# A closing phase of its own for the last graph, and four weight differences moved behind a norm

## The chip, the cores and the metric

The kernel runs on one core of one Trainium2 chip. The metric is the device time in microseconds (us) of one execution; the median of three runs is given. A profile is one further execution, taken by the hardware profiler, with a time of its own.

## What is computed

64 graphs of 256 nodes with 512 features pass two layers. Each layer normalizes its input, applies a relu, runs attention that a 256x256 mask per graph restricts, and adds the result to the input. Cut to what matters:

```python
h = relu(layernorm(x))                               # layer 0, 8 heads of 64
m = h @ map_w.T;  n = heads(m) / norm(heads(m))
q, k = heads(m @ q_w.T), heads(m @ k_w.T)
p = softmax(where(mask, NEG, q @ k.T / 8)) * keep
a = (n @ n.T > 0.1) * not_mask * p                   # "cosine" threshold
x = x + relu((a @ heads(h @ gcn_map_w.T)) @ gcn_W.T / (a.sum(-1) + 1))
h = relu(layernorm(x))                               # layer 1, 4 heads of 64
q, k, v = h @ Wq, h @ Wk, h @ Wv
x = x + (softmax(where(mask, q @ k.T / 8, -max)) @ v) @ Wo + bo
```

In layer 0 `mask` is where the adjacency is set (edges are taken out); in layer 1 only edges are kept. The softmax is computed without a maximum; sums are kept in `chk`, and at the end a branch takes a general path if one is out of bounds. With these inputs it is not taken.

## The kernel before, in words

All work on a graph is on whole tiles of 128 partitions, with keys on partitions and queries along the row, so that attention needs no transposes. The order of instructions on each engine is the order of the calls in the source: nothing is moved by a scheduler. Every engine works off its own queue in that order and waits for the others by semaphores.

`period(i)` is one step of a software pipeline over the graphs. In it stand, woven together: layer 1's attention of graph i-1 (called `b`), layer 0's attention and layer 1's norm and q, k, v of graph i (`g`), layer 0's products of graph i+1 (`nx`) and the normalized, transposed input of graph i+2 (`n2`). A loop runs `period` for i from 0 to 64. In period 63 there is no `nx`, and in period 64 only `b`, graph 63, is left.

The parts that the change and the prediction's steps touch:
- `products` (L404) makes scores on TensorE, `exps` (L411) exponentials on ScalarE (ACT), two banks of PSUM per pair of heads, from a ring of eight banks. `masked` multiplies by the mask on VectorE (DVE), L420 for layer 0 and L418 (edges) for layer 1.
- `halves` (L424) adds the two halves of a row of exponentials on GpSimd (POOL) to `d`, so that the sum product on TensorE has half the length.
- `units` (L387) makes unit vectors `nT`, for which the norms come back from DRAM; `cosines` (L441) makes their products, one triangle only. `far_off` masks by the threshold (L454, DVE), writes the off-diagonal block as `up` (L451, ACT) and has a DMA transpose it into `far` (L457); `far_back` masks the mirrored block by it (L466, DVE). `far_added` and `far_back` add both halves of the masked rows to `d` on POOL (L461, L468), but not for the last graph: there `sums` (L484) reads `d` and the two halves of `e`.
- `values` makes av (L431) and its relu (L474). `sums` gives `sms` by an ACT copy with a running sum (L486). `sums_back` transposes it (rt, L492) and takes reciprocals (L494); `heads_back` transposes avs (p_l), scales (L507) and adds to `xs` on POOL (L509).
- `moments` (L197 to L200), `deviations` (L203: root on ACT, then L204) and `normalized` (L210) are the second norm; `turned` transposes xn (p_t, L219) and writes hT with a relu (L220). L674 brings back the ACT table of the exponential.
- `queries_keys1` makes layer 1's q and k by seven half-size products (p_qk, L279), whose left factors POOL adds (L257 to L260) and whose results DVE adds (L304, L324); `values_in` makes v (p_v, L523).
- Of layer 1's attention: `sums1` (zb, L542) gives the softmax's denominators, one row per head; their reciprocals (L547) go through DRAM (`by_head`: by_rz, then `own`) to stand on all 64 partitions of a head; `values1` makes av1 (copied by L532), `divided` multiplies (L551), `result` makes p_o (L556) and adds it (L557); then the graph is stored.

The seven products need differences of weight blocks, which `finish_seven` makes in place by four DVE subtractions:

```python
sub(t[:, 5], t[:, 2], t[:, 3])      # L88
sub(t[:, 3], t[:, 3], t[:, 0])      # L89
sub(t[:, 4], t[:, 2], t[:, 3])      # L90
sub(t[:, 6], t[:, 1], t[:, 4])      # L91
```

For layer 1's weights `wqk1` this is called in period 0, behind the far blocks and ahead of the values of graph 0.

Of the kernel before, what the change touches and what calls it, by code (L numbers as in the profile page):

```python
# [150 lines left out]
def fast_path(ctx, tc, a, w, chk, out):  # L151
# [30 lines left out]

    def load(i):
        g = Graph()
        g.i, g.last, g.e, g.d, g.far = i, i == B - 1, {}, {}, {}
        g.xs = io.tile([P, NT, D], F32, tag="xs", name=f"xs{i}")
        nc.sync.dma_start(out=g.xs, in_=x_t[i])
        g.ad = io.tile([P, NT, S], U8, tag="ad", name=f"ad{i}", bufs=3)
        nc.sync.dma_start(out=g.ad, in_=adj_t[i])
        return g  # L190
# [194 lines left out]
    def units(g):  # L385

        nc.vector.tensor_mul(g.nT, g.nT, g.mT)  # L387
# [68 lines left out]
        g.far[c] = sb2.tile([P, 2, P], BF16, tag="far", name=f"far{g.i}_{c}", bufs=4)  # L456
        nc.sync.dma_start_transpose(out=g.far[c], in_=up.rearrange("p s q -> p (s q)"))  # L457

    def far_added(g, c):
        if not g.last:  # L460
            nc.gpsimd.tensor_add(g.d[c], g.d[c], g.e[c][:, :, :S])  # L461

    def far_back(g, c):

        e = g.e[c][:, :, S:S + P]
        nc.vector.scalar_tensor_tensor(e, g.far[c], 0.0, e, op0=ALU.is_gt, op1=ALU.mult)  # L466
        if not g.last:
            nc.gpsimd.tensor_add(g.d[c], g.d[c], g.e[c][:, :, S:])  # L468

    def values(g, n):  # L470
        av = bank(f"av{g.i}_{n}")
# [1 line left out]
            weighed(av, c - 2 * n, g.sem, g.e[c], 2 * c)  # L473
        nc.scalar.activation(g.avs[:, 2 * n:2 * n + 2, :], av, AF.Relu)  # L474

    def sums(g):

        sm = bank(f"sm{g.i}", [P, S])
        for n in range(2):
            for m in range(1 + NT if g.last else 1):  # L480
                for k in range(4):
                    c, s = 2 * n + k // 2, k % 2
                    part = g.e[c][:, s, (m - 1) * S:m * S] if m else g.d[c][:, s, :]
                    nc.tensor.matmul(sm[32 * k:32 * (k + 1), :], w.two[:, n, :], part, start=(n == 0 and m == 0),  # L484
                                     stop=(n == 1 and m == (NT if g.last else 0)))
        nc.scalar.activation(g.sms, sm, AF.Copy, accum_out=chk[:, g.i, 0:1])  # L486

    def sums_back(g):

# [25 lines left out]
        g.q1T, g.k1T = qk[:, :NIC, :], qk[:, NIC:, :]  # L515
        return seven_products(left, w.wqk1, None, qk, f"p_qk1{g.i}")

    def values_in(g, t):
        if t == 0:
            g.v = sb1.tile([P, NT, INNER], F32, tag="v", name=f"v{g.i}")  # L520
            g.p_v = bank(f"p_v{g.i}", [P, NT, INNER])
        for c in range(NKC):
            nc.tensor.matmul(g.p_v[:, t, :], g.h1T[:, c, t * P:(t + 1) * P], w.wv1[:, c, :],  # L523
                             start=(c == 0), stop=(c == NKC - 1))
        if t == NT - 1:
            nc.vector.tensor_copy(g.v, g.p_v)

    def values1(b):
        av = bank(f"av1_{b.i}")
        for c in range(NIC):  # L530
            weighed(av, c, b.v, b.e1[c], 2 * c)
        nc.scalar.copy(b.avs1, av)  # L532

    def sums1(b):

        zb = bank(f"zb{b.i}", [P, S])
        last = NT - 1 if b.last else 0
        for m in range(last + 1):
            for h in range(H1):
                c, s = divmod(h, 2)  # L540
                part = b.e1[c][:, s, m * S:(m + 1) * S] if b.last else b.d1[c][:, s, :]
                nc.tensor.matmul(zb[32 * h:32 * (h + 1), :], w.ones[:, :32], part, start=(m == 0), stop=(m == last))  # L542
        own = sb1.tile([P, 2, NIC, S], F32, tag="qk1", name=f"own{b.i}")
        b.avs1, b.z = own[:, 0], own[:, 1]
        b.rz = sb1.tile([P, S], F32, tag="rz", name=f"rz{b.i}")
        nc.scalar.activation(b.rz, zb, AF.Copy, accum_out=chk[:, b.i, 2:3])
        nc.vector.reciprocal(b.rz, b.rz)  # L547
        by_head(b.rz, 32, b.z, f"rz{b.i}")

# [7 lines left out]
        nc.vector.tensor_add(b.xs[:, t, :], p, b.xs[:, t, :])  # L557

    def period(i):
        g = graphs.get(i) if i < B else None  # L560
        b, nx, n2 = graphs.get(i - 1), graphs.get(i + 1), graphs.get(i + 2)
        def off_edges(*cs):
            for c in cs if g else ():
                masked(g.e[c], g.mask, edges=False)

        def halved_sums(*cs):
            for c in cs if g else ():
                g.d[c] = halves(g.e[c], f"0_{i}_{c}")


        if b:
            b.e1 = [exps(products(b.k1T, b.q1T, c, f"sc1_{b.i}_{c}"), f"1_{b.i}_{c}") for c in range(NIC)]
        if g:
            for c in range(NKC):
                g.e[c] = exps(products(g.kT, g.qT, c, f"sc0_{i}_{c}"), f"0_{i}_{c}")
        if b:
            for c in range(NIC):
                masked(b.e1[c], b.mask, edges=True)
            if b.last:
                for t in range(NT):  # L580
                    values_in(b, t)
        if nx:
            m, s = mapped(nx), messages(nx)
            next(m)
            next(s)

        off_edges(0, 1)
        halved_sums(1, 0)
        if b and not b.last:
            b.d1 = [halves(b.e1[c], f"1_{b.i}_{c}") for c in range(NIC)]  # L590
        if g:
            units(g)
        if nx:
            next(m)
        off_edges(2)
        halved_sums(2)
        if nx:
            next(m)
            next(s)
            next(m)  # L600
            halved(nx)

        if g:
            for c in range(NKC):
                far_off(g, c, cosines(g, c))
                if c == 0:
                    off_edges(3)
                    halved_sums(3)
            for c in range(NKC):
                far_added(g, c)  # L610
        if n2:
            shifts(n2, f"0_{n2.i}")
        if nx:
            q = queries(nx)
            next(q)
            next(s)
        if n2:
            sent(n2, f"0_{n2.i}", 0)
        if nx:
            next(q)  # L620
            squares(nx)
            next(s)
        if n2:
            sent(n2, f"0_{n2.i}", 1)
        for c in range(NKC):
            if nx and c < 3:
                next((q, s, q)[c])
            if g:
                far_back(g, c)
        if nx:  # L630
            lengths(nx, norms(nx))

        if i == 0:
            w.finish_seven(w.wqk1)
        if b:
            sums1(b)
            values1(b)
        if g:
            g.avs = sb1.tile([P, NKC, S], F32, tag="wide", name=f"avs{i}")
            g.sms = sb1.tile([P, S], F32, tag="sms", name=f"sms{i}")  # L640
            values(g, 0)
            values(g, 1)
            sums(g)
        if n2:
            joined(n2, f"0_{n2.i}")
            join(n2, 0)
        if nx:
            k = keys(nx)
            next(k)
        if b:  # L650
            nc.scalar.activation(b.rz, b.rz, AF.Copy, accum_out=chk[:, b.i, 3:4])
        if g:
            sums_back(g)
            heads_back(g)
        if n2:
            join(n2, 1)
        if nx:
            next(k)
        if n2:
            edges(n2)  # L660
        if b:
            divided(b)
        if g:
            moments(g, f"1_{i}")
        if nx:
            next(k)
        if g:
            deviations(g)
        if g:
            normalized(g, f"1_{i}")  # L670
        if nx:
            nc.scalar.activation(nx.rn, nx.rn, AF.Sqrt)

        nc.scalar.activation(spare[:, 1:], spare[:, :1], AF.Exp)  # L674
        if b:
            for t in range(NT):
                result(b, t)
                if b.last:
                    nc.sync.dma_start(out=out_t[b.i][:, t], in_=b.xs[:, t])
            if not b.last:  # L680
                nc.sync.dma_start(out=out_t[b.i], in_=b.xs)
        if i + 3 < B:
            graphs[i + 3] = load(i + 3)
        if g:
            g.h1T = turned(g, f"1_{i}", "wide")
            j = queries_keys1(g)
            for t in range(NT):
                nc.gpsimd.tensor_add(g.xs[:, t, :], g.xs[:, t, :], w.bo_b)
        if nx:
            next(k)  # L690
        if g:
            next(j)
        if nx:
            nc.vector.reciprocal(nx.rn, nx.rn)
            spread(nx)
        if g:
            next(j)
        if g:
            next(j)
            if not g.last:  # L700
                values_in(g, 0)
            next(j)
        if n2:
            n2.left_h = left_factors(n2.hT, "sh", n2.i)
        if i + 3 < B:
            moments(graphs[i + 3], f"0_{i + 3}")
        if g and not g.last:
            values_in(g, 1)

    def normal_input(g):  # L710
        g.hT = turned(g, f"0_{g.i}", "hT")
# [2 lines left out]
    with tc.manual_schedule():  # L714
# [54 lines left out]
            graphs[1].left_h = left_factors(graphs[1].hT, "sh", 1)  # L769
        if B > 2:  # L770
            moments(graphs[2], "0_2")
        for i in range(B + 1):
            period(i)


@with_exitstack
# [295 lines left out]
```

## Time and profile before

| | us |
|---|---|
| median of 3 runs | 3650.06 (3648.68 to 3650.47) |
| the profiled execution | 3652.85 |
| its span, first to last instruction | 3651.0 |
| PE busy in the span | 3613.9 (99%) |
| DVE, POOL, ACT busy | 2680.1, 2229.8, 1902.7 |
| weight loads (PEld) busy | 3088.9 |

The span is what the trace covers; the rest of the execution's time lies around it. PE is TensorE's products, PEld its weight loads, which run beside them. A row of the timeline gives start, length, engine, line, operation, tiles and number of instructions merged; in brackets, how long the engine had been idle just before and what released it. "PEclk" is the share of full speed that the throttle granted to TensorE. In a table of stretches, "(x…)" behind a busy time is the number of instructions. Every fp32 product stands in the trace as two records.

The middle periods are alike. The end of the program differs: period 63 begins near 3576 us of the span, period 64 near 3624 us.

### The profile page before, as it was taken

Reading aid. Unit: us, or ns where it says so; the run is one execution under the profiler, and the core shown is the slowest. Engines: PE = TensorE matmul, PEld = TensorE weight load, DVE = VectorE, ACT = ScalarE, POOL = GpSimd, SP = SyncE. Lnnn points to the kernel's source line nnn. Section 1 sums busy time; section 2 is a strip of 40 time slices with the busy share of each in tenths; the row PEclk is TensorE's granted clock in tenths of the full one; section 3 lists DMA queues with packets and bytes.
Section 4 is the critical chain, followed back from the end, with each engine's and each line's share of the span. In section 5 each row is a group of like instructions: output and inputs, shape, how many; then the busy total and the mean of one; then the engine's idle time right before and its main releaser. Section 6 shows DMA issues by size and latency. Waiting matters only on the chain.

```text
span 3651.0 us, 76421 instructions
## 1 busy us (share of the span) xinstructions
PE 3613.9 (99%) x29153; PEld 3088.9 (85%) x29153; DVE 2680.1 (73%) x5287; ACT 1902.7 (52%) x4481; POOL 2229.8 (61%) x2050
## 2 busy tenths in 40 slices
PE   8999999999999999999999999999999999999997
PEld 7888888888888888888888888888888888888885
DVE  7777777777777777777777777777777777777774
ACT  4555555555555555555545555555555555555542
POOL 4656656566566566665665666656656666566562
PEclk9999999999999999999999999999999999999998
DMA  4121121111211211211112112111121121211211
GB/s 118 44 57 44 55 56 46 55 51 50 57 44 55 61 42 54 53 50 56 45 54 61 44 52 57 46 56 45 53 61 44 53 57 47 55 45 54 60 32 33
DMA packets 358928, 191.73 MB, mean 53 GB/s; under 512 B 270336, under 2 KB 324896, under 8 KB 358560
## 3 DMA queue, kind: packets, MB, share of 16 engines
q1 hardware_dynamic: 357824, 186.24, 18.9%
q8 instruction: 233, 3.82, 0.4%
q14 instruction: 135, 1.11, 0.1%
q10 hardware_dynamic: 544, 0.52, 0.0%
q0 software_dynamic: 192, 0.04, 0.0%
HBM read 94.67 MB, written 34.34 MB: 35 GB/s over the span
## 4 chain that ended last, share of the span: by engine, by line
PE 97%; DVE 1%; DMA 1%; POOL 0%; issue 0%; ACT 0%; SPq 0%; ACTq 0%; DVEq 0%; POOLq 0%
PE sc L404 9%; PE av L431 9%; PE p_q L279 7%; PE p_m L279 7%; PE p_qk L279 6%; PE p_k L279 6%; PE p_o L556 6%; PE p_v L523 6%; PE p_s L274 6%; PE co L441 5%; PE p_qk_z L279 5%; PE p_m_z L279 5%; PE p_q_z L279 5%; PE p_k_z L279 5%; PE p_s_z L274 4%; PE sm L484 2%
## 5 line engine op out<-in xcount | busy, mean ns | idle before, releaser
L424 POOL TENSOR_TENSOR d<-e 128x512 f32<-128x512 f32 x382 | 595.7, 1584 | 366.2 <-DVE e L420 366.2
L411 ACT ACTIVATE e<-sc 128x512 f32<-128x512 f32 x768 | 383.3, 652 | 383.1 <-PE sc L404 376.8
L468 POOL TENSOR_TENSOR d<-d,e 128x512 f32<-128x512 f32 x252 | 322.8, 1291 | 171.4 <-DVE e L466 171.4
L509 POOL TENSOR_TENSOR xs<-xs,o 128x512 f32<-128x512 f32 x128 | 188.0, 1491 | 341.1 <-DVE o L507 341.1
L257 POOL TENSOR_TENSOR sh<-hT 128x256 f32<-128x256 f32 x128 | 93.3, 729 | 479.4 <-ACT hT L220 288.5
L420 DVE TENSOR_TENSOR e<-e,mask 128x1024 f32<-128x1024 f32 x256 | 378.8, 1500 | 0.0
L454 DVE SCALAR_TENSOR_TENSOR e<-co,e 128x256 f32<-128x256 f32 (+1 forms) x1024 | 287.8, 346 | 64.5 <-ACT up L451 35.4
L461 POOL TENSOR_TENSOR d<-d,e 128x512 f32<-128x512 f32 x252 | 312.5, 1272 | 0.0
L451 ACT ACTIVATE up<-co,below 128x128 bf16<-128x128 f32 x512 | 159.9, 363 | 186.2 <-PE co L441 180.4
L556 PE MATMUL p_o<-wo,own 128*128 128x512 f32 x512 | 236.1, 605 | 9.8 <-DVE own L551 9.8
L523 PE MATMUL p_v<-wv,hT 128*128 128x256 f32 x1024 | 242.2, 380 | 0.0
L431 PE MATMUL av<-e,sem 128*64 128x256 f32 x2048 | 232.4, 379 | 1.2 <-DVE e L466 1.2
L404 PE MATMUL sc<-qT,kT 64*128 64x256 f32 x2048 | 231.8, 377 | 0.0
L404 PEld LDWEIGHTS sc<-qT,kT 64*128 64x128 f32 x2048 | 198.4, 187 | 22.8 <-ACT hT L220 0.3
L494 DVE RECIPROCAL r<-rt 128x16 f32<-128x16 f32 x64 | 16.5, 258 | 268.5 <-PE rt L492 268.5
L431 PEld LDWEIGHTS av<-e,sem 128*64 128x64 f32 x2048 | 146.7, 137 | 76.1 <-DVE e L466 2.1
L523 PEld LDWEIGHTS p_v<-wv,hT 128*128 128x128 f32 x1024 | 185.1, 191 | 20.0 <-issue 0.3
L234 ACT ACTIVATE xn<-xs,shift,rs 128x512 f32<-128x512 f32 x124 | 100.5, 810 | 192.9 <-POOL d L461 190.4
L197 DVE BATCH_NORM_STATS2 st<-xs 128x6 f32<-128x512 f32 x256 | 173.9, 679 | 25.1 <-POOL xs L509 21.7
L466 DVE SCALAR_TENSOR_TENSOR e<-far,e 128x256 f32<-128x256 bf16 x256 | 190.3, 763 | 0.0
L441 PE MATMUL co<-nT 64*128 64x256 f32 (+1 forms) x2048 | 186.4, 332 | 2.8 <-ACT e L411 2.8
L556 PEld LDWEIGHTS p_o<-wo,own 128*128 128x128 f32 x512 | 94.5, 195 | 105.7 <-issue 102.4
(203 smaller groups left out, 9346.3 us busy)
## 6 DMA issues: line engine op xcount, KB each, us to landing
xs<-in_x_dram SPq DMA_DIRECT2D x64, 512.0 KB
nT<-by_rn SPq DMA_DIRECT2D x128, 256.0 KB
out_dram<-xs SPq DMA_DIRECT2D x63, 512.0 KB
own<-by_rz SPq DMA_DIRECT2D x128, 128.0 KB
ad<-in_adj_dram SPq DMA_DIRECT2D x64, 64.0 KB
far<-up SPq DMA_TRANSPOSE x256
turn<-flat SPq DMA_TRANSPOSE x248
mask<-adb SPq DMA_TRANSPOSE x128
```

Source lines behind the costliest of these rows:

```text
L274: nc.tensor.matmul(region, src[:, c, :], wt[:, block, c, :], start=p not in opened, stop=True, skip_group_check=True)
L279: nc.tensor.matmul(region[:, f, :], wt[:, block, c, f * P:(f + 1) * P], src[:, c, :], start=p not in opened, stop=True, skip_group_check=True)
L404: nc.tensor.matmul(ps[s][:, j, :], rows[h, c, j * P:(j + 1) * P], cols[h, c, :], start=True, stop=True)
L411: nc.scalar.activation(e[:, s, :], p.rearrange("p j q -> p (j q)"), AF.Exp, scale=SCALE)
L420: nc.vector.tensor_mul(e, e, m)
L424: nc.gpsimd.tensor_add(d, e[:, :, :S], e[:, :, S:])
L431: nc.tensor.matmul(av[s * DH:(s + 1) * DH, n, :], vs[:, j, (h0 + s) * DH:(h0 + s + 1) * DH], q[:, s, j * S:(j + 1) * S], start=(j == 0), s ...
L441: nc.tensor.matmul(ps[s][:, j, j * P:], g.nT[h, c, j * P:(j + 1) * P], g.nT[h, c, j * P:], start=(j == 0), stop=True, skip_group_check=True)
L461: nc.gpsimd.tensor_add(g.d[c], g.d[c], g.e[c][:, :, :S])
L468: nc.gpsimd.tensor_add(g.d[c], g.d[c], g.e[c][:, :, S:])
L523: nc.tensor.matmul(g.p_v[:, t, :], g.h1T[:, c, t * P:(t + 1) * P], w.wv1[:, c, :], start=(c == 0), stop=(c == NKC - 1))
L556: nc.tensor.matmul(p, b.avs1[:, c, t * P:(t + 1) * P], w.wo1[:, c, :], start=(c == 0), stop=(c == NIC - 1))
```

## The change

Three things change in the source:
- The loop runs `period` for i from 0 to 62, without its cases for missing graphs, and `closing()` follows. It does the work of periods 63 and 64: layer 0's attention of graph 63 (`g`), layer 1's of graph 62 (`b`) and then of graph 63, in an order of its own.
- `finish_seven(w.wqk1)` in period 0 stands behind `normalized(g)`.
- Helpers are cut differently (`sums` and `sums1` take a function that gives the parts to add, `inverted` and `own` are taken out of `sums1`, the copies of av1 and v go to the callers, `far_added` takes the half), with the same order of instructions in periods 1 to 62.

The diff's core:

```diff
-    def sums(g):
+    def sums(g, parts, name):
...
+        for c in range(NKC):
+            ps = parts(c)
+            for j, part in enumerate(ps):
+                for s in range(2):
+                    n, k = divmod(2 * c + s, 4)
+                    nc.tensor.matmul(sm[32 * k:32 * (k + 1), :], w.two[:, n, :], part[:, s, :],
+                                     start=(n == 0 and j == 0), stop=(n == 1 and j == len(ps) - 1))
+        return sm
...
-        if i == 0:
-            w.finish_seven(w.wqk1)
...
+        normalized(g, f"1_{i}")
+        if i == 0:
+            w.finish_seven(w.wqk1)
...
+    def closing():
+        g, b = graphs[B - 1], graphs.get(B - 2)
+        for c in range(NKC):
+            g.e[c] = exps(products(g.kT, g.qT, c, f"sc0_{g.i}_{c}"), f"0_{g.i}_{c}")
+        units(g)
+        co = [cosines(g, c) for c in range(2)]
+        for c in range(NKC):
+            masked(g.e[c], g.mask, edges=False)
+        se = sums(g, lambda c: both(g.e[c]), "se")
+        for c in range(2):
+            far_off(g, c, co[c])
+        first = sb1.tile([P, S], F32, tag="rn", name="first")
+        nc.scalar.activation(first, se, AF.Copy, accum_out=chk[:, g.i, 0:1])
+        for c in range(2, NKC):
+            far_off(g, c, cosines(g, c))
+        if b:
+            b.e1 = [exps(products(b.k1T, b.q1T, c, f"sc1_{b.i}_{c}"), f"1_{b.i}_{c}") for c in range(NIC)]
+        for c in range(NKC):
+            far_back(g, c)
+        if b:
+            for c in range(NIC):
+                masked(b.e1[c], b.mask, edges=True)
+        g.avs = sb1.tile([P, NKC, S], F32, tag="wide", name=f"avs{g.i}")
+        values(g, 0)
+        values(g, 1)
+        nc.scalar.activation(spare[:, 1:], spare[:, :1], AF.Sqrt)
...
+        nc.vector.tensor_add(g.sms, sums(g, lambda c: both(g.e[c]), "sm"), first)
+        sums_back(g)
+        heads_back(g)
+        if b:
+            sums1(b, lambda c: both(b.e1[c]))
+            own(b, "kT")
+            av = values1(b)
+        moments(g, f"1_{g.i}")
+        deviations(g)
+        if b:
+            nc.scalar.copy(b.avs1, av)
+        normalized(g, f"1_{g.i}")
+        nc.scalar.activation(spare[:, 1:], spare[:, :1], AF.Exp)
+        if b:
+            inverted(b)
+        g.h1T = turned(g, f"1_{g.i}", "wide")
+        j = queries_keys1(g)
...
+        next(j)
+        next(j)
+        next(j)
+        values_in(g, 0, (0, 1))
+        next(j)
+        values_in(g, 0, (2, 3))
+        g.e1 = [exps(products(g.k1T, g.q1T, c, f"sc1_{g.i}_{c}"), f"1_{g.i}_{c}") for c in range(NIC)]
+        values_in(g, 1)
+        nc.scalar.copy(g.v, g.p_v)
+        if b:
+            nc.scalar.activation(b.rz, b.rz, AF.Copy, accum_out=chk[:, b.i, 3:4])
+            divided(b)
+        for c in range(NIC):
+            masked(g.e1[c], g.mask, edges=True)
+        if b:
+            result(b, 0)
+        z = bank("z")
+        for c in range(NIC):
+            for j, part in enumerate(both(g.e1[c])):
+                for s in range(2):
+                    nc.tensor.matmul(z[s * DH:(s + 1) * DH, c, :], w.ones, part[:, s, :], start=(j == 0),
+                                     stop=(j == NT - 1))
+        spent = sb2.tile([P, NIC, S], F32, tag="xn", name="spent")
+        nc.scalar.activation(spent, z, AF.Copy, accum_out=chk[:, g.i, 2:3])
+        av = values1(g)
+        own(g, "qT")
+        for t in range(NT):
+            q = slice(t * P, (t + 1) * P)
+            nc.vector.reciprocal(g.z[:, :, q], z[:, :, q])
+            nc.vector.tensor_mul(g.avs1[:, :, q], av[:, :, q], g.z[:, :, q])
+        nc.scalar.activation(spent, g.z, AF.Copy, accum_out=chk[:, g.i, 3:4])
+        if b:
+            result(b, 1)
+            nc.sync.dma_start(out=out_t[b.i], in_=b.xs)
+        for t in range(NT):
+            result(g, t)
+            nc.sync.dma_start(out=out_t[g.i][:, t], in_=g.xs[:, t])
```

In the closing the last graph's denominators of layer 1 are made on all 64 partitions of each head at once (`z`, with 64 columns of ones), so they need no trip through DRAM. Layer 0's sum is made of two parts: `se`, of the edge-masked exponentials before the threshold, and `sm`, after it.

## The prediction

> **What bounds the kernel now.** I read the 40 slices first, then the chain that ended last, then the busy times by stage, then the timeline of the two places that the edit touches. The slices and the chain:
>
> ```profile
> PE   8999999999999999999999999999999999999997
> PEclk9999999999999999999999999999999999999998
> PE 97%; DVE 1%; DMA 1%; POOL 0%; issue 0%; ACT 0%; SPq 0%; ACTq 0%; DVEq 0%; POOLq 0%
> ```
>
> TensorE sets the time everywhere but in the last slice. Stage by stage (length, then PE, PEld, DVE, ACT, POOL busy, PEclk, DMA share, GB/s):
>
> ```profile
> 3456.00:3512.00 56.00, 56.00 (x456) 47.96 (x455) 41.49 (x83) 29.79 (x70) 34.84 (x33) 1.00 0.20 52
> 3568.00:3600.00 32.00, 26.55 (x226) 21.07 (x228) 20.56 (x35) 11.75 (x28) 14.34 (x11) 0.95 0.10 26
> 3600.00:3625.00 25.00, 20.14 (x128) 14.24 (x121) 10.48 (x22) 8.26 (x19) 8.20 (x8) 0.86 0.09 32
> 3625.00:3651.00 26.00, 11.77 (x53) 5.75 (x51) 7.13 (x11) 1.72 (x7) 0.00 (x0) 0.77 0.10 33
> ```
>
> A middle period is 56.0 us with PE full: nothing is to be had there. The last 75 us hold 16.5 us of idle PE, and part of the rest ran at half clock. The order of instructions on each engine is the same in both kernels except in period 0 and from the last graph's scores on, so only these two can move. The end of before:
>
> ```profile
> 3583.47 10.29 POOL L424 TENSOR_TENSOR d<-e 128x512 f32<-128x512 f32 x6 [11.41 <-DVE e L420]
> 3592.55 2.39 DVE L454 SCALAR_TENSOR_TENSOR e<-co,e 128x256 f32<-128x256 f32 x8 [1.32 <-POOL d L424]
> 3605.63 6.68 PE L556 MATMUL p_o<-wo,own 128*128 128x512 f32 x8 [2.43 <-DVE own L551]
> 3612.84 1.09 ACT L220 ACTIVATE hT<-p_t 128x512 f32<-128x512 f32 x2 [3.24 <-PE p_t L219]
> 3629.08 1.75 DVE L547 RECIPROCAL rz<-rz 128x256 f32<-128x256 f32 x1 [0.90 <-ACT rz L546]
> 3636.49 0.69 DVE L551 TENSOR_TENSOR own<-own 128x512 f32<-128x512 f32 x1 [2.63 <-DMA own<-by_rz]
> 3637.32 6.18 PE L556 MATMUL p_o<-wo,own 128*128 128x512 f32 x8 [7.00 <-DVE own L551]
> ```
>
> Three things make the end long: six half-sums on POOL that DVE's threshold masks wait for; graph 62's p_o standing on PE ahead of graph 63's transposes, at half clock; and graph 63's last normalization through DRAM (7.0 us of idle PE), after which p_o is at half clock again. The clock, read from PE alone (length, PE busy, clock):
>
> ```profile
> 82.27:85.69 3.42, 1.18 (x12) 1.00 0.09 22
> 85.69:89.10 3.41, 3.41 (x16) 0.50 0.54 162
> 3601.42:3604.83 3.41, 1.31 (x10) 1.00 0.18 60
> 3604.83:3608.24 3.41, 2.61 (x3) 0.50 0.00 0
> 3608.24:3611.65 3.41, 3.41 (x5) 0.50 0.03 5
> 3628.72:3632.13 3.41, 1.60 (x16) 1.00 0.00 1
> ```
>
> A stretch of 3.41 us with 1.2 or 1.3 us of PE work is followed by half clock, one with 1.6 is not; 2.6 busy us did not bring the full clock back, 3.4 did.
>
> **Part 1, weight differences in period 0.**
>
> ```profile
> 73.11 3.00 POOL L468 TENSOR_TENSOR d<-d,e 128x512 f32<-128x512 f32 x2 [0.43 <-DVE e L466]
> 73.55 1.43 DVE L88 TENSOR_TENSOR wqk<-wqk 128x512 f32<-128x512 f32 x1
> 75.01 1.64 DVE L89 TENSOR_TENSOR wqk<-wqk 128x512 f32<-128x512 f32 x1
> ```
>
> Alone one such subtraction takes 0.69 us (L90, L91); beside POOL's two sums the first two take twice that, and the sums take 3.00 us where period 62's take 2.56. PE's last sum product waited for that POOL result (0.64 us), and rt, the heads, the norm and the transposes follow it. Moved behind xn, the four run beside nothing of POOL: 4 x 0.69 = 2.8 us, from 85.5 to 88.3. Their reader is the second half of p_qk, at about 89.7. The kT additions behind them on DVE wait for p_k_z until 89.3, so they are not delayed. Gain 3.00 - 2.56 = 0.44 us; the bounds are 0 and 0.64 (the whole PE wait), and below nothing up to 1 us if p_k_z comes early. I take 0.44.
>
> **Part 2, the closing phase.** All times on before's clock; the anchor is 3576.41, where PE takes up scores. The half-sums (POOL 10.3 us), 8 products on d, and the last DRAM trip (3 DMAs) go; 16 products se, one ACT copy, one DVE addition, 8 products z, two reciprocals and two ACT copies come.
> - PE: scores of 63 first, 32 records, 3.62 us, to 3580.1. ACT's eight exps at 0.50 us (12 took 5.99) run from 3577.7 to 3581.85. nT had landed at 3576.0, so units (1.22) end at 3578.5, under the first exps. Four masks at 1.2 us follow ACT: to 3583.5. POOL is idle, so they stay at 1.2.
> - Cosines 0, 1 (half of 2.89): 3580.1 to 3581.5. se waits for the last mask. Eight sm products take 1.07 us (two records each), eight 64-row av products 1.95. The new order puts two products of one output group close together; I take 2.1 us for 16 if groups overlap across chunks, 3.4 if only pairs do. se ends at 3584.4, cosines 2, 3 at 3585.85, scores of 62 at 3587.7 (2.0 in before; here 1.85).
> - DVE: 16 threshold masks, 1.15 us a chunk, 3583.5 to 3588.1. The four DMA transposes of `far` land 2.36 us after their `up` and 1.25 to 1.35 us apart in before: the last at 3589.6. Four far_back (0.355) end at 3590.05; av starts with chunk 0 at 3588.65 and takes 3.62: 3592.3. Before's av ended at 3598.56. Behind the wait for `far` on DVE stand the two edge masks of 62 (2.4 us, to 3592.4), whose reader zb comes at 3596.4: covered by 4 us.
> - sm 2.1: 3594.4. The DVE addition stands where ACT's copy stood (0.42 for 0.38): rt at 3595.05 against 3601.89. Gain so far 6.84.
> - From rt to the first xn before needs 6.43 us; without L551 beside POOL's xs (2.93 instead of 2.5) about 6.1: 3601.15, xn done at 3601.65. PE meanwhile does p_l, zb, av1 of 62, to 3599.65, then idles 2.15 us. ACT takes the root at 3600.55, then the copy of av1 (0.58), the Exp table (1.28) and `spare` (0.2): hT cannot start before 3602.85, though p_t is done at 3602.3. Before: 3612.84. Gain 9.99; graph 62's p_o, 6.68 us, is no longer in the way.
> - The Trainium skill's page "ScalarE: Activation LUTs", section "What ACT_TABLE_LOAD costs", puts a switch of sets at about 2.66 us, a load plus a drain. The row here is 1.28 us, and the next ACTIVATE starts 0.01 us after it. By the page hT would start 1.4 us later; I go by the row.
> - From hT (X = 3602.85) p_qk runs as before to X+6.2. Before then lost 0.78 us for L324 and 1.10 us for the additions; two halves of p_v (0.9 each) fill these. Scores X+9.25 to X+11.25, p_v 1.8, p_o of 62 for t=0 1.72 to X+14.8. Exps end at X+12.5, edge masks at X+14.0. In DVE's queue `divided(62)` stands ahead of these masks and waits for by_rz: the reciprocal ends at 3603.9, and the trip takes 5.3 to 5.6 us, so it lands at X+6.5, before DVE gets there at X+9.1.
> - z (8 products, 1.8) to X+16.6, av1 to X+18.4. ACT's copy of z, to X+17.45, holds the first reciprocal (its wait names ACT). Two reciprocals: 128x256 took 1.74. First to X+19.2, product 0.41, second to X+21.45, product to X+21.9. PE does p_o of 62 (t=1) and of 63 (t=0) beside them; p_o for t=1 runs X+22.05 to X+23.8. DVE has two additions and the 0.29 + 0.42 of the check first: last addition ends at X+24.75. In before the span ended 6.67 us after it (3644.30 to 3650.97)[...]. The 512 KB store of 62 now goes 1 us ahead of 63's stores; 512 KB took 1.6 us of transfer, landed 2.8 us after the issue. That is hidden in the 6.67.
> - End: 3602.85 + 24.75 + 6.67 = 3634.3. Gain 16.7; with part 1, 17.1.
>
> **Clock.** The page "TensorE: Matmul & The Clock Gate", section "HAM oscillation — how this bites in real kernels", warns of idle gaps above some 3.4 us. The closing has none (2.15 us at most), so by the page the gain stays 17.1. The rows say otherwise: gaps of 2.2 and 2.4 us were enough. From 3598.4 to 3601.85 the closing has 1.25 us of work, so half clock is likely in p_t and p_qk. One stretch costs 1.4 us (part of it beside ACT), two cost 2.7. I go by the rows and one stretch: 17.1 - 1.4 = **15.7 us**.
>
> The profiled execution of before is 3652.85 us, its span 3651.0, so 1.85 lies around the span; the sum gives 3637.1 for such a run. The median of the runs is 2.79 below the profiled one: 3650.06 - 15.7 = **3634.4**.
>
> **Rivals.**
> - Full clock: no low stretch. For it, a 2.15 us gap can fall across two stretches; against it, the two rows. 3633.0, or 3631 if the ACT copy of z does not hold the reciprocal.
> - More waits: sm takes 3.4 (+1.3) and two low stretches come (+1.3): gain 13.1, 3637.0; with the table switch of the page, 3638.4.
> - The new waits take most of the gain. DVE's one queue carries masks of both graphs; if a DMA wait (`far`, `own`) lands 10 us later than in before, gain 6 us, 3644. The landing times speak against it.
> - Slower: the clock stays at half through the closing. From 3584.4 to the last p_o PE has about 35 us of work; doubled it ends at 3655, 11 us after before's 3643.5, so some 3661. It decides when more than 17.1 us of PE work run at half clock without cover; the longest low piece in the trace is 6.83 us.
> - The order is not changed as said: the instruction order shows it is.
>
> **Chances.** Likeliest 0.47; full clock 0.22; more waits 0.24; most of the gain gone 0.05; slower 0.02. A measurement of this kernel can tell about 0.2%, 7.3 us, from no change. The first three cases are faster (0.93), the fourth the same (0.05), the last slower. The range reaches from the best case, 3630.5, to 3640.5, which takes in both bounds of sm, table and clock.
>
> **What would show it.** Right: no POOL d in the closing; av of 63 ends near 3592; hT near 3603; one half-clock stretch around p_t and p_qk; no DVE wait for `own`; last addition about 24.8 us after hT; in period 0 two POOL sums in 2.56 us. Wrong: PE waits between cosines and av above 2 us, sm above 3 us, DVE idle behind a DMA, p_qk waiting for wqk, or p_o at half clock at the end.

## The result and the profile after

The changed kernel takes 3634.38 us (median of 6 runs, 3633.81 to 3635.01), the kernel before 3649.74 us (6 runs, 3648.51 to 3650.47): a ratio of 0.9958, 95% interval 0.9946 to 0.9971, or 15.4 us less. The forecast was 3634.4 us. The profiled execution takes 3633.84 us, its span is 3632.1 us.

The rows of the clock and of the chain that ended last, for the changed kernel (the last digit of the clock was 8 before):

```profile
PEclk9999999999999999999999999999999999999999
PE 98%; DVE 1%; DMA 0%; ACT 0%; issue 0%; POOL 0%; SPq 0%; DVEq 0%; ACTq 0%; POOLq 0%
```

The end of the changed kernel by stretches (length, PE, PEld, DVE, ACT, POOL busy, PEclk, DMA share, GB/s):

```profile
3568.00:3600.00 32.00, 28.73 (x271) 20.92 (x270) 22.43 (x48) 14.74 (x35) 4.79 (x4) 0.99 0.11 26
3600.00:3625.00 25.00, 24.68 (x139) 16.98 (x137) 12.78 (x18) 6.61 (x17) 5.27 (x6) 0.94 0.06 21
3625.00:3632.07 7.07, 0.27 (x1) 0.08 (x1) 1.11 (x3) 0.00 (x0) 0.00 (x0) 0.88 0.32 121
```

In the second stretch PE is full up to the last p_o. In the kernel before, 26 us with 11.8 us of PE work still followed. The timeline of the closing:

```profile
3576.97 4.63 DVE L420 TENSOR_TENSOR e<-e,mask 128x1024 f32<-128x1024 f32 x4 [0.41 <-ACT e L411]
3581.52 2.20 DVE L454 SCALAR_TENSOR_TENSOR e<-co,e 128x256 f32<-128x256 f32 x8
3584.00 2.21 DVE L454 SCALAR_TENSOR_TENSOR e<-co,e 128x256 f32<-128x256 f32 x8 [0.28 <-ACT up L451]
3589.77 1.96 PE L481 MATMUL sm<-e,two 128*32 128x256 f32 x32
3598.60 1.28 ACT L733 ACT_TABLE_LOAD   x1
3599.04 1.45 PE L219 MATMUL p_t<-ident,xn 128*128 128x128 f32 x8 [2.49 <-DVE xn L210]
3599.90 0.20 ACT L733 ACTIVATE spare<-spare 128x1 f32<-128x1 f32 x1
3600.01 1.11 ACT L220 ACTIVATE hT<-p_t 128x512 f32<-128x512 f32 x2
3600.64 3.17 PE L279 MATMUL p_qk<-hT,wqk 128*128 128x128 f32 x16 [0.15 <-ACT hT L220]
3618.42 1.76 DVE L769 RECIPROCAL own<-z 128x256 f32<-128x256 f32 x1 [1.98 <-ACT spent L764]
3625.04 0.69 DVE L565 TENSOR_TENSOR xs<-p_o,xs 128x512 f32<-128x512 f32 x1 [0.36 <-PE p_o L564]
```

DVE goes from mask to mask without a wait for POOL, sm takes 1.96 us, ACT is not idle ahead of hT (no bracket), and the last addition ends 25.7 us after hT began. The PE rows around the last norm (length, PE busy, clock, DMA share, GB/s) show the one half-clock stretch of this execution before its end:

```profile
3596.20:3599.62 3.42, 0.93 (x9) 1.00 0.00 0
3599.62:3603.03 3.41, 3.25 (x16) 0.50 0.00 1
```

Period 0 of the changed kernel:

```profile
73.24 2.56 POOL L460 TENSOR_TENSOR d<-d,e 128x512 f32<-128x512 f32 x2 [0.43 <-DVE e L465]
87.76 1.10 DVE L91 TENSOR_TENSOR wqk<-wqk 128x512 f32<-128x512 f32 x1
89.00 1.13 PE L279 MATMUL p_qk<-hT,wqk 128*128 128x128 f32 x8 [0.77 <-DVE wqk L91]
```

POOL's sums take 2.56 us, as period 62's did before, and p_qk now waits 0.77 us for the last difference (L91). That one took 1.10 us instead of 0.69, while POOL's L257 ran from 87.26 to 88.31 us.

Three lengths of the end, in the two traces:

| us | before | predicted | after |
|---|---|---|---|
| first score product to first hT | 36.43 | 26.44 | 25.38 |
| hT to the end of the last addition | 31.46 | 24.75, and 1.4 for the clock | 25.72 |
| last addition to the end of the span | 6.67 | 6.67 | 6.34 |

### The profile page after: what moved, and what is told of

It reads as the page before. It is cut to its first block, busy times and chain, and to the rows that moved or that the text cites. A ratio compares the mean times of both kernels' runs of the same rounds, so it can differ in the third digit from the quotient of the medians.

```text
span 3632.1 us, 76457 instructions
## 1 busy us (share of the span) xinstructions
PE 3608.6 (99%) x29177; PEld 3083.9 (85%) x29177; DVE 2677.7 (74%) x5289; ACT 1904.7 (52%) x4481; POOL 2221.8 (61%) x2044
## 4 chain that ended last, share of the span: by engine, by line
PE 98%; DVE 1%; DMA 0%; ACT 0%; issue 0%; POOL 0%; SPq 0%; DVEq 0%; ACTq 0%; POOLq 0%
PE sc L404 9%; PE av L431 9%; PE p_q L279 7%; PE p_m L279 7%; PE p_k L279 7%; PE p_qk L279 6%; PE p_v L527 6%; PE p_s L274 6%; PE p_o L564 6%; PE co L441 5%; PE p_qk_z L279 5%; PE p_q_z L279 5%; PE p_m_z L279 5%; PE p_k_z L279 5%; PE p_s_z L274 5%; PE sm L481 2%
## 5 line engine op out<-in xcount | busy, mean ns | idle before, releaser
L424 POOL TENSOR_TENSOR d<-e 128x512 f32<-128x512 f32 x376 | 585.7, 1584 | 354.4 <-DVE e L420 354.4
L257 POOL TENSOR_TENSOR sh<-hT 128x256 f32<-128x256 f32 x128 | 93.8, 733 | 473.5 <-ACT hT L220 283.5
L441 PEld LDWEIGHTS co<-nT 64*128 64x128 f32 x2048 | 161.3, 187 | 19.5 <-issue 0.4
```

What stands on the lines that cost most here:

```text
L424: nc.gpsimd.tensor_add(d, e[:, :, :S], e[:, :, S:])
L441: nc.tensor.matmul(ps[s][:, j, j * P:], g.nT[h, c, j * P:(j + 1) * P], g.nT[h, c, j * P:], start=(j == 0), stop=True, skip_group_check=True)
```

## The experiments

Every experiment was timed beside the kernel before on the same chip, but not all on one chip. The medians of the kernel before range from 3649.52 to 3650.10 us over these chips, so a difference between two rows, or between a row and the changed kernel, is uncertain by some 0.6 us.

| | median us (runs) | ratio to before, 95% interval |
|---|---|---|
| e1 differences only | 3649.73 (13) | 1.0001, 0.9993 to 1.0010 |
| e2 closing only | 3634.08 (5) | 0.9955, 0.9942 to 0.9969 |
| e3 before, filled, products too wide | 3655.70 (20) | 1.0016, 1.0009 to 1.0022 |
| e4 closing, filled, products too wide | 3635.19 (5) | 0.9959, 0.9946 to 0.9973 |
| e5 before, filled | 3646.23 (20) | 0.9991, 0.9985 to 0.9998 |
| e6 closing, filled | 3633.31 (5) | 0.9958, 0.9944 to 0.9971 |
| e7 half-sums kept | 3638.76 (7) | 0.9970, 0.9959 to 0.9981 |
| e8 last norm by DRAM | 3640.99 (12) | 0.9977, 0.9969 to 0.9986 |
| e9 graph 62 first | 3637.80 (5) | 0.9966, 0.9953 to 0.9979 |
| e10 copies late | 3633.48 (5) | 0.9956, 0.9942 to 0.9969 |
| e11 closing tuned | 3633.18 (5) | 0.9953, 0.9940 to 0.9967 |
| e12 tuned, warm start | 3631.40 (5) | 0.9950, 0.9937 to 0.9964 |

**e1 and e2: each part alone.** e1 is the kernel before with this, e2 the changed kernel with the reverse:

```diff
-        if i == 0:
-            w.finish_seven(w.wqk1)
         if b:
             sums1(b)
...
             normalized(g, f"1_{i}")
+        if i == 0:
+            w.finish_seven(w.wqk1)
```

> The kernel before with only the weight differences moved behind the first norm. Theory A (POOL and DVE slow each other): POOL's last two sums of period 0 take 2.56 us instead of 3.00, later work starts 0.44 us earlier, and up to 0.8 us of it goes again where p_qk waits for the last difference: 0 to 0.5 us faster than before, 3649.3 to 3649.8. Rival: the position matters more, because half clock at the norm of period 0 goes with it: 1.7 us faster.

> The changed kernel with the weight differences back at their old place in period 0. Theory A: nearly all of the gain is the closing phase: 3634.4 to 3634.9, some 15 us faster than before, and POOL's two sums of period 0 take 3.00 us again. Rival: the two parts add up to more than each alone: 3636 or above.

The closing alone gives the whole gain, and the differences alone nothing that can be measured. One of e2's five executions took only 3631.69 us, at a granted clock that rounds to 1.000 (0.999 in the others); there is no trace of it. Why the differences give nothing shows in the traces. From the first p_k product of graph 0, ahead of the loop, to that of graph 2, in period 1 (the text put on record for e12 calls them p_k of period 0 and of period 2), it takes, by place of the differences and by the clock behind period 0's norm:

| us | full clock | half clock |
|---|---|---|
| old place | 106.40 (e3), 106.41 (e2), 106.43 (e5) | 108.04 (before), 108.05 (e11) |
| new place | 106.97 (after), 106.98 (e4, e6), 106.97 (e10) | 107.59 (e1, e9), 107.60 (e7), 107.61 (e8) |

The move gains 0.45 us where PE is at half clock and loses 0.56 us where it is not. The 0.44 us of POOL's sums are there in either case (graph 1's p_k comes 50.88 us after graph 0's, not 51.32), but at full clock p_qk is ready for the last difference before DVE is. In e2, with the differences at the old place and at full clock, p_qk runs through without a wait:

```profile
87.99 1.95 PE L279 MATMUL p_qk<-hT,wqk 128*128 128x128 f32 x16
```

From graph 1's p_k to the p_qk_z behind p_qk it takes 12.55 us in e2 and 13.56 us in the changed kernel: 1.01 us lost against 0.44 gained.

The gap of 2.2 us ahead of p_t is in all of these. Whether half clock follows depends on where it falls. All changes of the clock in one trace lie a whole number of steps of 3.413 us apart. In before such a stretch ends at 85.69 us and holds the whole gap, with 1.18 us of PE work. In the changed kernel, counted back from the half clock at 3599.62 us, a border lies at 83.89 us, in the middle of the gap, and both stretches keep more work:

```profile
80.47:83.89 3.42, 2.66 (x24) 1.00 0.01 2
83.89:87.30 3.41, 1.94 (x18) 1.00 0.31 45
```

**e3 and e5: the kernel before, kept at full clock.** Products of no use fill idle PE time:

```diff
+    def warm(name, n):
+        p = bank(name, [P, S])
+        for _ in range(n):
+            nc.tensor.matmul(p, w.ident, w.bc[:, :S], start=True, stop=True)
...
+            if g.last:
+                warm("warm0", 6)
...
+            if g.last:
+                warm("warm1", 5)
...
+            if b.last:
+                warm("warm2", 16)
```

The first six stand ahead of graph 63's cosines, the five behind its p_l, the sixteen behind its av1.

e3 had them 512 wide. Counted as 0.43 us each, they took 0.88: a product stands as two records of some 0.44 us. The last 16 took 14.0 us and stood in front of p_o, so e3 does not answer its question: what the clock gives and what the products cost are mixed in it.

> The kernel before with idle PE time of its last two periods filled by products of no use (6 ahead of the last graph's cosines, 5 behind its p_l, 16 behind its last av1; 0.43 us each), so that PE's clock stays at full speed. Theory A (order and waits give most of the gain): both p_o go from 6.7 and 6.2 us to 3.5 us, but the first waits are as before: 5 to 6 us faster than before, 3644 to 3645. Rival (the gain is the clock's): 12 us or more faster, 3638 or below. If the products of no use come late and stand in the way, it shows as PE waits behind them.

> The kernel before with products of no use in the idle PE time of its last two periods, now 256 columns wide (0.43 us each; the 512 wide ones of the earlier run took 0.88 and stood in the way): 6, 5 and 16 of them. Theory A (order and waits give most of the closing's gain): the two p_o take 3.5 us each, graph 63's hT and the end come 5 to 6 us earlier than before, 3644 to 3645. Rival (the gain is the clock's): 3638 or below.

In e5 the two p_o of the kernel before, 6.68 and 6.18 us there, run at full clock:

```profile
3604.41 3.67 PE L556 MATMUL p_o<-wo,own 128*128 128x512 f32 x8 [0.36 <-DVE own L551]
3633.04 3.60 PE L556 MATMUL p_o<-wo,own 128*128 128x512 f32 x8
```

From graph 63's hT to `bad`, the last DVE instruction, it takes 29.73 us instead of 32.37, and hT comes 2.49 us earlier: 5.1 us between the two traces, as expected, but 3.3 us between the medians, so the expected 3644 to 3645 us were missed by 1.2 us. One half-clock stretch remains in e5 too (av of graph 62 takes 3.63 us, not 1.95). Between e5 and e6 (below), both nearly free of half clock, the time from graph 63's p_k to `bad` differs by 12.8 us in the traces. So order and waits are most of the gain; the rival, that it is the clock's, falls.

**e4 and e6: the closing kept at full clock.**

```diff
             av = values1(b)
+        warm = bank("warm", [P, S])
+        for _ in range(5):
+            nc.tensor.matmul(warm, w.ident, w.bc[:, :S], start=True, stop=True)
         moments(g, f"1_{g.i}")
```

e4 had them 512 wide: they took 4.56 us in a gap of 2.5 us, and p_t came 1.8 us late behind them. So e4's time (3635.19 us, not the expected 3633.3 to 3633.8) does not decide, though p_qk took 2.05 us and no half clock came before the end.

> The changed kernel with five products of no use (0.43 us each) in the 2.5 us of idle PE ahead of the last graph's transposes. Theory A (a 3.41 us stretch with about 1.2 us of PE work brings half clock): the stretch of half clock in p_t and p_qk is gone, p_qk takes 1.95 to 2.05 us instead of 3.17, and the time is 3633.3 to 3633.8 in every execution, about 1 us below the upper of the two values that the changed kernel shows. Rival (by the skill's rule only idle gaps above 3.4 us cost clock): no change, 3634.4, with both values.

> The changed kernel with five products of no use, now 256 wide (2.15 us in a gap of 2.5 us). Theory A (half clock follows a stretch of 3.41 us with little PE work, the gap being 2.5 us): p_qk takes 2.05 us, not 3.17, no half clock before the end, 3633.0 to 3633.8 in all executions. Rival (gaps below 3.4 us cost no clock, as the skill's rule has it): 3634.4 and no change in p_qk.

```profile
3596.90 2.43 PE L730 MATMUL warm<-bc,ident 128*128 128x256 f32 x10
3601.06 2.05 PE L279 MATMUL p_qk<-hT,wqk 128*128 128x128 f32 x16 [0.52 <-ACT hT L220]
```

In e6 hT stands where it did (46.94 us after graph 63's p_k in both traces), p_qk takes 2.05 us, and from hT to `bad` it takes 25.52 us instead of 26.63. The stretch of half clock cost 1.1 us in the changed kernel's trace; in e2's trace, where it covers more of p_qk (27.00 us from hT to `bad`), it cost 1.5 us. The median is 1.07 us lower. The idle gap that brought it was 2.5 us. Not all executions fall within the expected 3633.0 to 3633.8 us: two of five took 3633.99 and 3634.16. Period 0's clock, worth 0.6 us, and the start of the program (see "What stays open") are left alone here.

**e7: half-sums on POOL kept for graph 63.**

```diff
-        se = sums(g, lambda c: both(g.e[c]), "se")
+        for c in range(NKC):
+            g.d[c] = halves(g.e[c], f"0_{g.i}_{c}")
...
-        nc.vector.tensor_add(g.sms, sums(g, lambda c: both(g.e[c]), "sm"), first)
+        nc.scalar.activation(g.sms, sums(g, lambda c: [g.d[c]] + both(g.e[c]), "sm"), AF.Copy, ...)
```

> The changed kernel with graph 63's half-sums on POOL and the one sum product of 24 as in the kernel before, in place of se and sm. Theory A: the four half-sums slow DVE's masks and hold the threshold masks back, but graph 62's two are no longer ahead of them: 1 to 2 us slower than the changed kernel, 3635.4 to 3636.4. Rival (POOL's half-sums were the main thing, 4 us or more): 3638 or above.

```profile
3577.33 6.77 DVE L420 TENSOR_TENSOR e<-e,mask 128x1024 f32<-128x1024 f32 x4 [0.41 <-ACT e L411]
3578.64 7.82 POOL L424 TENSOR_TENSOR d<-e 128x512 f32<-128x512 f32 x4 [8.01 <-DVE e L420]
3584.78 4.28 PE L404 MATMUL sc<-qk 64*128 64x256 f32 x16 [3.45 <-DVE e L454]
3588.99 4.74 PE L431 MATMUL av<-e,sem 128*64 128x256 f32 x32
```

4.4 us slower than the changed kernel, where 1 to 2 were expected; the rival's "4 us or more" holds. Beside POOL the four masks take 6.77 us instead of 4.63. PE, its cosines done, waits 3.45 us for DVE's first threshold mask, which frees the bank of PSUM that graph 62's scores go to. It then runs at half clock for 6.8 us, and av takes 4.74 us instead of 3.62 (e9). The single sum of 24 products ends 3.2 us behind av, 1.3 us later than sm's 16. So these 4.4 us are the half-sums with the clock that their wait costs. hT comes 4.78 us later; behind it nothing changes.

**e8: the last normalization through DRAM.**

```diff
-        z = bank("z")
...
+        sums1(g, lambda c: both(g.e1[c]))
+        own(g, "qT")
+        inverted(g)
+        nc.scalar.copy(g.avs1, values1(g))
+        nc.scalar.activation(g.rz, g.rz, AF.Copy, accum_out=chk[:, g.i, 3:4])
+        divided(g)
```

> The changed kernel with graph 63's last normalization through DRAM again (zb, one reciprocal, three DMAs), in place of z and two reciprocals. Theory A: the trip takes 5.5 us, graph 62's last p_o covers 1.7 of it, and the two p_o of graph 63 run at half clock behind the idle time: 5 to 6 us slower than the changed kernel, 3639.4 to 3640.4. Rival (the reciprocals on all partitions cost nearly what the trip does): within 2 us of the changed kernel.

```profile
3623.75 0.69 DVE L559 TENSOR_TENSOR own<-own 128x512 f32<-128x512 f32 x1 [2.38 <-DMA own<-by_rz]
3624.59 5.95 PE L564 MATMUL p_o<-wo,own 128*128 128x512 f32 x8 [4.86 <-DVE own L559]
```

6.6 us slower in the medians, a little more than the 5 to 6 expected, and 5.28 us more from hT to `bad` in the traces (6.4 against e6, which like e8 has no half clock at p_qk). PE idles 4.86 us, and the two p_o behind it are at half clock for 4.6 us. The two reciprocals on all partitions, 3.5 us, beat a trip of 5.4.

**e9: graph 62's attention first.** Its scores and masks open the closing; zb, reciprocal, trip and av1 stand ahead of graph 63's values; and

```diff
-        if b:
-            inverted(b)
+        if b:
+            for t in range(NT):
+                result(b, t)
+            nc.sync.dma_start(out=out_t[b.i], in_=b.xs)
         g.h1T = turned(g, f"1_{g.i}", "wide")
```

> The changed kernel with graph 62's attention back ahead of graph 63's, as in the kernel before: its scores and edge masks first, zb, the reciprocal, the DRAM trip and av1 ahead of graph 63's values, p_o ahead of graph 63's transposes. se, sm and z stay. Theory A: graph 63's chain is the one that sets the end; it comes 5 to 7 us later at hT, of which 1.7 us come back behind it: 4 to 6 us slower than the changed kernel, 3638.4 to 3640.4. Rival (the order of the two graphs does not matter, PE has the same work): within 1.5 us.

```profile
3600.84 5.40 PE L564 MATMUL p_o<-wo,own 128*128 128x512 f32 x8 [2.43 <-DVE own L559]
3606.71 1.09 ACT L220 ACTIVATE hT<-p_t 128x512 f32<-128x512 f32 x2 [1.90 <-PE p_t L219]
```

3.4 us slower, a little below the 4 to 6 expected. hT comes 6.09 us later, as expected, with p_t behind a p_o that is partly at half clock; but 2.91 us come back behind it, not 1.7: neither p_o of graph 62 is there any more, and p_qk is at full clock.

**e10: two copies late.**

```diff
-        if b:
-            nc.scalar.copy(b.avs1, av)
         normalized(g, f"1_{g.i}")
...
         g.h1T = turned(g, f"1_{g.i}", "wide")
+        if b:
+            nc.scalar.copy(b.avs1, av)
...
-        nc.scalar.activation(spent, z, AF.Copy, accum_out=chk[:, g.i, 2:3])
...
+        nc.scalar.activation(spent, z, AF.Copy, accum_out=chk[:, g.i, 2:3])
         nc.scalar.activation(spent, g.z, AF.Copy, accum_out=chk[:, g.i, 3:4])
```

> The changed kernel with two ACT copies moved: av1 of graph 62 behind graph 63's hT (it stood between the root and the table load), and the copy of z behind the two reciprocals (they waited for it). Theory A: hT starts 0.5 us earlier, unless xn and p_t come last there, and the first reciprocal starts 0.6 us earlier: 3633.2 to 3633.8. Rival (neither copy ends a wait that sets the time): 3634.4.

```profile
3600.77 1.08 ACT L220 ACTIVATE hT<-p_t 128x512 f32<-128x512 f32 x2
3618.83 1.76 DVE L767 RECIPROCAL own<-z 128x256 f32<-128x256 f32 x1 [1.20 <-PE z L761]
```

The reciprocal now waits for PE's z, no longer for ACT's copy: that wait was real. hT starts 0.30 us earlier against graph 63's p_k, of 0.5 expected: now p_t, no longer the table load, comes last. The median is within the expected values, 0.9 us below the changed kernel's; but the runs of the two overlap (3633.20 to 3634.91), so the time alone settles nothing. e11, whose closing is at full clock, shows it better: 71.90 us from graph 63's p_k to `bad` against e6's 72.45.

**e11 and e12: a version from these results.** e11 has both copies late, e6's fill, and the differences at the old place. e12 adds

```diff
+        if i == 0:
+            p = bank("warm0", [P, S])
+            for _ in range(5):
+                nc.tensor.matmul(p, w.ident, w.bc[:, :S], start=True, stop=True)
         g.h1T = turned(g, f"1_{i}", "wide")
```

> Both copies late, five 256-wide products of no use ahead of the transposes, and the weight differences of period 0 at their old place. Theory A: 0.5 to 1.1 us from the copies, 1 us from the clock in those executions that had half clock, 0 to 0.5 us from period 0: 3632.0 to 3633.2, faster than both kernels. Rival (gains of this size are lost to other waits): 3634 or above.

> The tuned closing of the run before (copies late, products of no use ahead of the last transposes, differences at their old place) with five more products of no use, 256 wide, in the 2.2 us of idle PE ahead of period 0's transposes. Theory A (the old place costs less at full clock, and the half clock of period 0 is one more case of a stretch with little PE work): from p_k of period 0 to p_k of period 2 it takes 106.4 us, as in the traces with the old place and full clock, never 108.05; median 3631.5 to 3632.5. Rival (half clock in period 0 does not come from that gap): 3633.2 as in the run before.

e11 lies at the upper end of the expected 3632.0 to 3633.2 us. Its profiled execution had half clock in period 0 and took 108.05 us from graph 0's p_k to graph 2's. In e12 that is 106.41 us (131.59 - 25.18), all five runs lie within 0.6 us (3631.24 to 3631.81), and the trace has no half clock before the last instruction of DVE. PE in e12 behind the fill:

```profile
87.27 1.95 PE L279 MATMUL p_qk<-hT,wqk 128*128 128x128 f32 x16
```

So e12, at 3631.40 us, is faster than both kernels: 3.0 us below the changed kernel, whose runs it does not overlap. The two were not timed on one chip, but the medians of the kernel before beside them agree within 0.1 us (3649.81 and 3649.74).

## Why the prediction was right, and where not

**The number was right, its two parts not equally.** The closing gave all of the 15.4 us. Part 1, put at 0.44 us, is zero on the average. Two of its steps failed. "Moved behind xn, the four run beside nothing of POOL": L257 ran beside the last one and made it 0.4 us longer. "Their reader is the second half of p_qk, at about 89.7": that was read from an execution in which p_t and p_k_z ran at half clock. At full clock the reader is at 88.2, DVE is done at 88.9, and p_qk waits. This wait for wqk was among the prediction's own signs of being wrong. Where period 0 has half clock, the gain of 0.44 us came true (0.45); where it has not, the lower bound, "below nothing up to 1 us if p_k_z comes early", did.

**First score to hT**: 25.38 us for a predicted 26.44. Av ended 15.2 us in, predicted 15.9: a chunk of threshold masks took 1.10 us, not 1.15, and the longest wait for a `far` was 0.6 us. sm took 1.96 of the predicted 2.1, which fits products of one group that overlap across chunks; the bound of 3.4 is out. Root, copy, table load and `spare` stand on ACT as worked out, and hT waited for them. The table load cost 1.28 us, and `spare` began 0.02 us after it, as the row said; the 2.66 us of the Trainium skill's page "ScalarE: Activation LUTs" (section "What ACT_TABLE_LOAD costs") did not appear.

**hT to the end**: 25.72 us where 24.75 + 1.4 were put. Without the clock the sum is closer still: in e6 it is 24.60 us for 24.75. One stretch of half clock came where it was expected, behind a stretch with 0.93 us of PE work and a gap of 2.5 us; it cost 1.1 us in this trace and 1.5 us in e2's. By the warning of gaps above some 3.4 us in the Trainium skill's page "TensorE: Matmul & The Clock Gate" (section "HAM oscillation — how this bites in real kernels") there would have been no loss here; the rows of before were the better guide. The waits of 0.78 and 1.10 us read for the kernel before are of weight loads; PE itself idled 0.59 and 0.94 us there, which changes nothing in the sum.

**From trace to median.** The forecast took a gain worked out on one profiled execution off the median. In the traces the kernels differ by 18.9 us (3651.0 to 3632.1). The closing is 17.1 us shorter (74.56 to 57.44), more than the 15.3 predicted for it, and 1.8 us lie ahead of it. From graph 0's p_k to graph 2's it takes 1.07 us less, some 0.6 of them clock. From there to graph 63's p_k it takes 0.85 us less: 3421.42 us in before, 3420.56 to 3420.58 us in all other traces; why is not known. The start took 0.14 us more. The medians differ by only 15.4 us, since the profiled execution of before was 3.1 us above its median: e1's trace, with the same end of program, lacks the 0.85 us and is 2.0 us shorter at the end, with one half-clock stretch in the first p_o instead of two. So the forecast holds two errors that nearly cancel: the gain worked out, 15.7 us, was 3.3 us below the 19.0 us between the two profiled executions (3652.85 and 3633.84), and these 19.0 us are 3.6 us above the gain of the medians. That it meets the median within 0.1 us is luck: no run of the changed kernel took 3634.4 us.

**Which causes carry it.** Undone one at a time in the closing: the DRAM trip 6.6 us, POOL's half-sums 4.4, graph 62's place 3.4. They sum to 14.4 of 15.4; each of them carries some half clock of its own, so this is not a clean division.

**The rivals fell.** Not full clock: one low stretch came. Not more waits: sm stayed under 2.1 us. Not new waits: DVE did not wait for `own`. Not slower: the low stretch was 3.41 us long.

**What stays open.** The changed kernel's six runs fall on two values, 3633.8 and 3634.95, three each. Three things vary between traces. Half clock in period 0 costs 0.6 us, and its form in p_qk (3.17 to 3.58 us) up to 0.4 us. The start of the program varies more: graph 0's p_k, behind the first loads of weights, begins between 25.18 and 26.59 us. The changed kernel (3633.84 us) and e10 (3634.91 us):

```profile
25.53 1.95 PE L279 MATMUL p_k<-mT,wk 128*128 128x128 f32 x16
26.59 1.95 PE L279 MATMUL p_k<-mT,wk 128*128 128x128 f32 x16
```

These 1.06 us are nearly the whole difference between the two executions, 1.07 us. Which of the three splits the six runs into two values can't be told without a trace of each.

## What to carry to other kernels

At the end of a software pipeline, where no next item fills the gaps, it pays to write out the last item's own order: its chain first, the work that is left of the item before it placed into the gaps, and trips that the steady state hides replaced by direct work. Judge a moved step in an execution at full clock too: a reader that seems late may be late only because PE was slow. Where PE has a gap of two to three us ahead of dense work, a few products of no use, sized by the time that a trace shows for them, can buy back the half clock.

## What the hardware showed that was not expected

- Half clock came behind stretches of 3.41 us with 0.92 to 1.31 us of PE work at gaps of 2.2 to 2.8 us (0.92 is the one ahead of graph 63's cosines in before). From 15 us of the span on, in all 14 traces, every stretch at full clock with at most 1.51 us of work was followed by half clock (1.51 is e11's last one), and none with 1.60 us or more. Filling the gap took it away at the norms of period 0 and of the closing (e6, e12).

```profile
3580.94:3584.35 3.41, 0.92 (x10) 1.00 0.00 0
3623.02:3626.43 3.41, 1.51 (x4) 1.00 0.74 289
```

- Beside POOL's sums, a DVE mask of 128x1024 took 1.69 us instead of 1.16, and POOL 1.96 us for one sum instead of 1.28 (e7).
- A wait on ACT's copy of z held DVE's reciprocal of the same bank of PSUM: it began 0.82 us behind the end of z's last product (e10, with the copy moved away: 0.05 us). Both only read z; whether the two could read it at once, no run shows.
